# Regrouping the output stage, the edge features and the layer changes of a graph transformer layer

## The chip, the core and the metric

The program runs on one NeuronCore of one Trainium2 chip. The metric is the device time of one execution in microseconds, and a time stands for the median of several executions. All arithmetic is in float32.

## What is computed

One layer of a graph network over N = 3125 nodes with D = 256 features and 100,000 edges, cut here to what matters:

```python
xn = layernorm(x)
# graph part: one message for each edge, summed at its destination
m   = relu(concat(xn[src], edge_attr) @ W1.T + b1)      # edge_attr has 3 columns
hN  = segment_sum(m, dst, N)
gnn = l2norm(relu(concat(xn, hN) @ W2.T))
# mixer: four layers of linear attention and a feed-forward block
for l in range(4):
    h = layernorm(y) * g1 + b1
    q = softmax(h @ Wq, axis=features);  k = softmax(h @ Wk, axis=nodes)
    y = y + (q @ (k.T @ (h @ Wv))) @ Wo + bo
    y = y + gelu(layernorm(y) * g2 @ W1 + b1) @ W2 + b2
x = x + gnn + mix
# expert part: 16 experts, the best 2 for each node
z = layernorm(x)
moe = sum over the 2 best experts e of  gate_e * (relu(z @ w1_e + b1_e) @ w2_e + b2_e)
out = x + layernorm(z + moe) * gamma + beta
```

## The kernel before

Nodes are held as 25 tiles of 125 rows (`xm`, 125 partitions x 25 x 256). Most work runs over seven blocks of tiles, `BLOCKS`: five of 4 tiles, one of 3, one of 2. Block `NB - 1` is the last one.

**Prologue.** For each block the input is normalized (`stage_xn`), a copy in the attention's form is made on ACT (`stage_xh1`), the block is transposed and copied by ACT (`stage_xnT`), and projected by the node part of the edge weights (`stage_proj`), which is stored to `proj` in DRAM. Between these run the first layer's keys and queries.

**Mixer.** The letters of the stages recur in the prediction: `t1` transposes the normalized block, `k` and `q` are the key and query products with their softmax work on DVE and ACT, `ek` and `qT` transpose the exponentials of the keys and the queries, `m` adds the block to the sum `msum` of keys times values. Once all blocks are in `msum`, `context` builds one small matrix `mo` from it, by a chain of four products that depend on each other (mean, its transpose, `ctx`, `mo`). Then `y` adds `qT @ mo` to the nodes, `ln2` and `t2` normalize and transpose, `f1` and `f2` are the feed-forward products, and the next layer's attention stages of the blocks before are woven in. A *change of layer* below is the stretch from the last block's `f2` through `context` to the first `f1` of the next layer. There are four: change 0 (into layer 0, after the prologue), 1, 2 and 3 (into the last layer).

**Edges.** Edges are cut into 784 chunks of 128, and 98 groups of 8 chunks. For a group, GpSimd issues 8 indirect DMAs that gather rows of `proj` (`load_chunk`), SP loads the edge features `ea` in 4 small transfers; `message_step` multiplies the features by a 4-row weight `w1w` on four row strips of the array (8 products, each of 4 rows with 256 columns) and adds the result to the gathered rows (DVE), then Relu (ACT); `sum_step` sums the messages into windows of 32 destinations by a one-hot product and adds the windows of two groups ago to `hNT`. These three kinds of step (0, 1 and 2) stand in a list `due`, with a due place in groups. The list is worked off between the mixer's stages of the first three layers: each stage calls `worked(columns)`, which moves `place` on by `columns * (NG + 1 + LEAD) / total` and runs what has become due. Before a gather, `worked` may issue a one-element copy (`tick`) on GpSimd that waits for the stage's output. Calls of `worked(12 * D)` at a change of layer move `place` without any product of the mixer's own.

PE, ACT and POOL run in the order in which the program is written in the mixer (`manual_schedule`); DVE and SP are ordered by the scheduler.

**Last layer and routing.** The graph part's update (`stage_g`, weights `w2x` and `w2n`) and the gates are woven in. The `slots` tables are written by indirect DMAs.

**Experts.** 37 tiles, 16 of 128 slots and 21 of 256, each with its own expert's weights from SP; each result is scattered by GpSimd to `outs` in DRAM.

**Output.** `outs` is read back in seven parts (four tiles each, then one), the first choice by SP and the second by ACT, each part in two transfers (`by_parts`, 112 and 13 partitions). Identity products on PE sum the two, DVE takes the statistics, and the reciprocal root is worked out in 11 small DVE instructions (`finish_stats`). ACT normalizes, DVE multiplies by gamma, GpSimd adds `xm`, and SP stores. The order on each engine is the scheduler's.

## Time and profile before

| what | value |
|---|---|
| median of 3 runs | 1988.45 us (1987.17 to 1989.06) |
| profiled execution | 1994.73 us, its span 1993.0 us |
| mean granted clock of TensorE | 0.953 |
| PE busy | 1807.7 us, 91% of the span |
| DVE busy | 1165.1 us, 58% |
| POOL busy | 1126.5 us, 57% |
| ACT busy | 743.6 us, 37% |

The span is the time from the first to the last instruction of the profiled execution. Busy is the time in which an engine had an instruction under way; times in which POOL starts a transfer but shows nothing are not in it. The granted clock is TensorE's, as a share of full speed. By stages: the prologue ends at about 130 us, the four changes of layer lie at about 130 to 190, 530 to 650, 950 to 1020 and 1360 to 1420 us, the edges are worked off between 134 and 1363 us, the experts run from about 1690 to 1920 us, and the output stage from 1928 us to the end.

### The profile page before, as it was taken

The numbers are of one execution on the slowest core, as the hardware profiler recorded it, in microseconds if no ns is written. First come the engines' busy times: TensorE is split into PE (matmuls) and PEld (weight loads), VectorE is DVE, ScalarE is ACT, GpSimd is POOL, SyncE is SP. The second block draws the span as 40 slices with busy tenths as digits, with TensorE's granted clock in tenths as the row PEclk, the third lists the DMA queues.
The fourth block names the chain that finished last, engine by engine and source line by source line (L and its number), as shares of the span: only waits on it lengthen the run. The fifth ranks groups of instructions, "written<-read, shape, count | busy, mean of one in ns | idle before, by whom it ended". The sixth has DMA issues, their size and how long they took to land. (4 is left out here: it accounts for less than half of the span.)

```text
span 1993.0 us, 30766 instructions
## 1 busy us (share of the span) xinstructions
PE 1807.7 (91%) x9749; PEld 1269.3 (64%) x9749; DVE 1165.1 (58%) x3761; ACT 743.6 (37%) x1343; POOL 1126.5 (57%) x1429
## 2 busy tenths in 40 slices
PE   6988999999888999999889999998999994999963
PEld 4764656666655666667546666666777783888841
DVE  7654566666664666766656666765646653333326
ACT  3543444344533444544333444443222231222202
POOL 1026777677667777777677777771114435545512
PEclk9998999999988999999889999999999996999987
DMA  6123333233433233334423233333211113777744
GB/s 188 66 77 92 89 85 88 79 88 93 129 98 91 84 93 91 89 84 127 118 81 89 85 90 87 89 89 100 67 29 29 28 19 116 241 259 260 273 130 120
DMA packets 83294, 210.74 MB, mean 106 GB/s; under 512 B 26523, under 2 KB 42306, under 8 KB 78389
## 3 DMA queue, kind: packets, MB, share of 16 engines
q0 software_dynamic: 44800, 118.16, 20.6%
q1 hardware_dynamic: 37246, 87.31, 13.9%
q10 hardware_dynamic: 1078, 3.20, 0.6%
q8 instruction: 84, 1.38, 0.3%
q14 instruction: 86, 0.70, 0.1%
HBM read 187.34 MB, written 21.19 MB: 105 GB/s over the span
## 5 line engine op out<-in xcount | busy, mean ns | idle before, releaser
L255 POOL DMA_INDIRECT gat<-proj,src_i x784 | 761.9, 972 | 212.4 <-issue 163.4
L581 PE MATMUL f_ps<-h2T,ww 128*128 128x500 f32 (+2 forms) x896 | 360.6, 551 | 6.4 <-ACT h2T L339 5.8
L299 ACT ACTIVATE gat<-gat 128x512 f32<-128x512 f32 x392 | 237.6, 630 | 341.0 <-DVE gat L298 315.4
L591 PE MATMUL f_ps<-ww,gT 128*125 128x256 f32 x1600 | 362.3, 382 | 0.0
L298 DVE TENSOR_TENSOR gat<-gat,pw 128x512 f32<-128x512 f32 x392 | 245.5, 680 | 162.1 <-PE pw L294 138.3
L591 PEld LDWEIGHTS f_ps<-ww,gT 128*125 128x125 f32 x1600 | 295.1, 188 | 58.4 <-issue 10.5
L581 PEld LDWEIGHTS f_ps<-h2T,ww 128*128 128x128 f32 x896 | 167.0, 192 | 168.5 <-issue 122.8
L583 ACT ACTIVATE gT<-f_ps,ffb 128x500 f32<-128x500 f32 (+2 forms) x224 | 135.6, 631 | 136.4 <-PE f_ps L581 135.8
L279 PE MATMUL pq<-gat,hot 128*32 128x256 f32 x1568 | 137.6, 405 | 22.4 <-ACT gat L299 22.3
L273 DVE TENSOR_TENSOR hNT<-hNT,win_ps 128x64 f32 x392 | 84.7, 216 | 74.4 <-PE win_ps L270 64.4
L925 POOL DMA_INDIRECT slots<-rec,at x50 | 59.5, 1189 | 110.0 <-DVE rs_u L113 63.7
L596 DVE TENSOR_TENSOR xm<-xm,f_ps 125x512 f32<-125x512 f32 (+1 forms) x52 | 34.7, 667 | 138.7 <-PE f_ps L591 136.4
L1120 PE MATMUL e_ps<-ew,hs 128*128 128x256 f32 x464 | 112.8, 381 | 2.2 <-DVE o L1124 2.2
L294 PE MATMUL pw<-w1w,ea 4*128 4x256 f32 x1568 | 114.6, 403 | 0.0
L1127 POOL DMA_INDIRECT outs<-o,ids x58 | 57.4, 989 | 100.6 <-DVE o L1125 97.5
L458 PE MATMUL q_ps<-wwq,hT 128*125 128x256 f32 x400 | 99.8, 402 | 4.6 <-DVE gat L298 3.6
L563 POOL TENSOR_TENSOR xm<-xm,b 125x1024 f32<-125x1024 f32 (+2 forms) x28 | 59.9, 2140 | 77.6 <-DVE xh L122 58.5
L547 PE MATMUL y_ps<-mo,qT 128*125 128x256 f32 x400 | 98.0, 397 | 4.9 <-DVE mo L538 4.9
L294 PEld LDWEIGHTS pw<-w1w,ea 4*128 4x128 f32 x1568 | 72.5, 185 | 45.0 <-issue 34.5
L495 PE MATMUL m_ps<-xh,ek 125*128 125x257 f32 x400 | 97.9, 398 | 1.8 <-ACT ek L481 1.8
L279 PEld LDWEIGHTS pq<-gat,hot 128*32 128x32 f32 x1568 | 49.6, 112 | 77.9 <-ACT gat L299 45.3
L1120 PEld LDWEIGHTS e_ps<-ew,hs 128*128 128x128 f32 x464 | 85.2, 190 | 20.4 <-issue 4.5
(222 smaller groups left out, 2652.8 us busy)
## 6 DMA issues: line engine op xcount, KB each, us to landing
ew<-ffn_w SPq DMA_DIRECT2D x37, 1154.0 KB
gat<-proj,src_i POOLq DMA_INDIRECT x784
ww<-mix_W SPq DMA_DIRECT2D x8, 1024.0 KB
ea<-eaT SPq DMA_DIRECT2D x392, 4.0 KB
ogs<-outs SPq DMA_DIRECT2D x6, 448.0 KB
ogs<-outs ACTq DMA_DIRECT2D x6, 448.0 KB
out<-ogs SPq DMA_DIRECT2D x6, 448.0 KB
xnT_d<-stage SPq DMA_DIRECT2D x5, 500.0 KB
```

What stands on the lines that cost most here:

```text
L255: nc.gpsimd.indirect_dma_start(out=gats[-1][:, (j // SC) % 2, j % SC, :], out_offset=None, in_=proj, in_offset=bass.IndirectOffsetOnAxis(a ...
L279: nc.tensor.matmul(pq[s * W:(s + 1) * W, :], hot[:, s * SC + i, :], gats[s // 2][:, s % 2, i, :], start=(i == 0), stop=(i == SC - 1))
L294: nc.tensor.matmul(pws[s][:, i, :], ea[s * W:s * W + 4, i * P:(i + 1) * P], w1w[s * W:s * W + 4, :], start=True, stop=True)
L298: nc.vector.tensor_add(msg, msg, pws[s])
L299: nc.scalar.activation(msg, msg, AF.Relu)
L458: nc.tensor.matmul(ps[:, i, :], hT[:, c, cols(o + i)], wt["Wq"][:, c, :], start=(c == 0), stop=(c == KC - 1))
L495: nc.tensor.matmul(ps, st["ek", b][:, i, c * P:(c + 1) * P], xh1s[b % 2][:, i, :], start=(i == 0), stop=(i == n - 1))
L547: nc.tensor.matmul(ps[:, i, :], qT[:, c, cols(t0 + i)], mo[:, c, :], start=(c == 0), stop=(c == KC - 1))
L581: nc.tensor.matmul(ps, wt["W1"][:, c, f * P:(f + 1) * P], st["h2T", b][:, c, :m], start=(c == 0), stop=(c == KC - 1))
L583: nc.scalar.activation(gT[:, f, :m], ps, AF.Gelu, bias=ffb[:, l, f:f + 1])
L591: nc.tensor.matmul(ps[:, i, :], st["gT", b][:, f, cols(o + i)], wt["W2"][:, f, :], start=(f == 0), stop=(f == NF - 1))
L1120: nc.tensor.matmul(ps[:, j, :], x["hs"][:, f, j * P:(j + 1) * P], x["w2"][:, f, :], start=(f == 0), stop=(f == NEF - 1))
```

## The change

It has four parts.

1. Output stage: all loads are issued by SP, in eight parts of 1, 2, 4, 4, 4, 4, 4 and 2 tiles; the root is one ACT instruction, with a reciprocal on DVE; the addition of `xm` goes from GpSimd to DVE; stores are issued by GpSimd; the order on PE, ACT and DVE is the written one, in which a part's multiply, add and store come after the next part's statistics.
2. A group's edge features come as one transfer of 128 x 128, laid out by the host. The two chunks of a strip share one product of 8 rows with 512 columns, whose weight is block-diagonal, so 4 products for a group in place of 8.
3. Order at changes of layer: the last block's `q` moves into `context` of the next layer, its `qT` behind `y` of block 1, and `qT` of the block before it behind `k` of the last. `place` stands still (`held`) from the last block's `f2` to the next layer's first `y`; in that stretch `fill(kind)` runs the next edge step of one kind at four places (from change 1 on), and `total` leaves these columns and the `worked(12 * D)` calls out. In the prologue `stage_xnT` comes ahead of `stage_xh1`.
4. The last expert's half tile is put behind its full tiles, and `w2n` gets a buffer of its own.

```diff
-                ea = edge.tile([P, SC * P], F32, name="ea")
-                for s in range(S):
-                    e0 = (g * S + s) * SC * P
-                    nc.sync.dma_start(ea[s * W:s * W + 4, :], a["eaT"][:, e0:e0 + SC * P])
+                ea = edge.tile([P, P], F32, name="ea")
+                nc.sync.dma_start(ea, a["ea_g"][g])
...
-            for i in range(SC):
-                for s in range(S):
-                    nc.tensor.matmul(pws[s][:, i, :], ea[s * W:s * W + 4, i * P:(i + 1) * P],
-                                     w1w[s * W:s * W + 4, :], start=True, stop=True)
+            for s in range(S):
+                nc.tensor.matmul(pws[s], ea[s * W:s * W + SC * 4, :], w1w[s * W:s * W + SC * 4, :],
+                                 start=True, stop=True)
...
-        total = (DEPTH - 1) * (attention + forward + 60 * D)
+        at_end = sum(len(r) * (2 * KC * TP + KC * D + 2 * KC * P + KC * (D + 1)) for r in BLOCKS[-2:])
+        total = (DEPTH - 1) * (attention + forward) - (DEPTH - 1) * (at_end + BT * KC * D)
+        held = False
...
-            if not spread:
+            if not spread or held:
...
+        def fill(kind):
+            while due and due[-1][1] in (0, kind):
+                _, k, step, i = due.pop()
+                step(i)
+                if k == kind:
+                    return
...
-        def context(l):
+        def context(l, between):
...
+            between[0]()
             ps = mm_tile("meanT_ps").rearrange("p (h m) -> p h m", h=KC)
...
+            between[1]()
             ps = mm_tile("ctx_ps")[:, :D].rearrange("p (c m) -> p c m", c=KC)
...
+            between[2]()
             ps = mm_tile("mo_ps").rearrange("p (c d) -> p c d", c=KC)
...
+            between[3]()
...
             stage_xn(0)
+            stage_xnT(0)
             stage_xh1(0)
-            stage_xnT(0)
...
+            stage_m(0, NB - 1)
             for l in range(last):
                 start_layer(l)
-                context(l)
+                more = (lambda kind: None) if l == 0 else fill
+                context(l, [lambda: stage_q(l, NB - 1), lambda: more(1), lambda: None, lambda: more(2)])
                 load(l + 1, "Wk", "Wq", "Wv")
                 stage_y(l, 0)
+                held = False
                 stage_ln2(0)
                 stage_y(l, 1)
-                worked(12 * D)
+                stage_qT(l, NB - 1)
                 stage_t2(l, 0)
-                worked(12 * D)
...
+                    if b == NB - 1:
+                        stage_ln1(b)
+                        held = True
+                        fill(2)
...
                 stage_ek(l + 1, NB - 2)
-                stage_qT(l + 1, NB - 2)
                 stage_t1(l + 1, NB - 1)
                 stage_m(l + 1, NB - 2)
                 stage_k(l + 1, NB - 1)
-                stage_q(l + 1, NB - 1)
+                stage_qT(l + 1, NB - 2)
                 stage_ek(l + 1, NB - 1)
-                if l + 1 < last:
-                    stage_qT(l + 1, NB - 1)
-                    stage_m(l + 1, NB - 1)
+                fill(1)
+                stage_m(l + 1, NB - 1)
...
-        w2n = wts.tile([P, KC, D], F32, tag="wq", name="w2n")
+        w2n = gates.tile([P, KC, D], F32, name="w2n")
...
-            order += [(i, False)] + [(j, True) for j in range(i * NFS // E, (i + 1) * NFS // E)]
+            full = [(j, True) for j in range(i * NFS // E, (i + 1) * NFS // E)]
+            order += [(i, False)] + full if i < E - 1 else full + [(i, False)]
...
+        def scales(r):
+            tt = slice(r[0], r[-1] + 1)
+            nc.scalar.activation(rs_v[:, tt], mv[:, tt, 1], AF.Sqrt, bias=eps[:, 0:1])
+            return tt
+
+        def normalized(r, tt):
+            nr = tmp.tile([TP, 4], F32, name="nr")
+            nc.vector.reciprocal(rstd[:, tt], rs_v[:, tt])
+            nc.vector.scalar_tensor_tensor(nr[:, :len(r)], mv[:, tt, 0], -1.0, rstd[:, tt], op0=ALU.mult,
                                            op1=ALU.mult)
             for i, t in enumerate(r):
-                nc.scalar.activation(ogs[:, 0, t, :], pss[i], AF.Identity, scale=rstd[:, t:t + 1],
+                nc.scalar.activation(ogs[:, 0, t, :], pss[t], AF.Identity, scale=rstd[:, t:t + 1],
                                      bias=nr[:, i:i + 1])
+
+        def stored(r, tt):
             ys = ogs[:, 0, tt, :]
-            nc.vector.tensor_mul(ys, ys, gamma[:TP, None, :].to_broadcast([TP, n, D]))
-            nc.gpsimd.tensor_add(ys, ys, xm[:, tt, :])
-            by_parts(nc.sync, ov[:, tt, :], ys)
+            nc.vector.tensor_mul(ys, ys, gamma[:TP, None, :].to_broadcast([TP, len(r), D]))
+            nc.vector.tensor_add(ys, ys, xm[:, tt, :])
+            by_parts(nc.gpsimd, ov[:, tt, :], ys)
+
+        with tc.manual_schedule(engines={mybir.EngineType.PE, mybir.EngineType.Activation, mybir.EngineType.DVE}):
+            last = None
+            for r in parts:
+                sums(r)
+                tt = scales(r)
+                if last:
+                    stored(*last)
+                normalized(r, tt)
+                last = r, tt
+            stored(*last)
```

## The prediction

> **What bounds the kernel now.** I read the page's busy times first, then busy time by stretches (columns: stretch, its length, busy time and instructions of PE, PEld, DVE, ACT, POOL, granted clock, DMA share, GB/s), then PE's waits in one change of layer, then the timeline of that change and of the output.

> ```profile
> PE 1807.7 (91%) x9749; PEld 1269.3 (64%) x9749; DVE 1165.1 (58%) x3761; ACT 743.6 (37%) x1343; POOL 1126.5 (57%) x1429
> ...
> 130.00:190.00 60.00, 45.80 (x232) 27.76 (x230) 30.60 (x90) 18.91 (x33) 39.40 (x50) 0.83 0.34 99
> 190.00:530.00 340.00, 329.45 (x1974) 220.15 (x1974) 211.44 (x634) 150.39 (x264) 249.28 (x348) 0.98 0.32 91
> 530.00:650.00 120.00, 98.94 (x566) 61.35 (x559) 71.44 (x222) 44.01 (x79) 80.76 (x107) 0.89 0.35 101
> 950.00:1020.00 70.00, 54.53 (x299) 33.18 (x298) 45.54 (x139) 25.23 (x48) 45.57 (x58) 0.83 0.33 94
> 1360.00:1420.00 60.00, 49.78 (x236) 41.28 (x235) 37.30 (x128) 16.05 (x30) 7.81 (x12) 0.94 0.28 85
> 1920.00:1993.00 73.00, 24.11 (x52) 10.36 (x52) 36.83 (x148) 11.80 (x25) 15.00 (x8) 0.70 0.50 134
> ```

> PE bounds the mixer: between changes of layer it is 97% busy at clock 0.98. At the four changes it idles and its clock falls. The idle is 14.2 + 21.1 + 15.5 + 10.2 = 61 us; busy time at a lower clock, summed over stretches of 10 us, adds 7.7 + 11.1 + 8.9 + 2.3 = 30. So the changes lose 91 us, and the last 73 us of the span hold only 24 us of PE work.

> ```profile
> PE qT_ps L144 <- DVE qs L469: 9.0, 2, 4.9
> PE f_ps L581 <- ACT h2T L339: 4.6, 1, 4.6
> PE pq L279 <- ACT gat L299: 4.0, 4, 2.0
> PE y_ps L547 <- DVE mo L538: 2.1, 1, 2.1
> PE h2T_ps L144 <- DVE xh L122: 1.4, 1, 1.4
> ...
> 574.43 6.64 PE L547 MATMUL y_ps<-mo,qT 128*125 128x256 f32 x16 [2.09 <-DVE mo L538]
> 582.22 3.72 PE L547 MATMUL y_ps<-mo,qT 128*125 128x256 f32 x16
> ```

> These are PE's waits in change 1 (total, times, longest). The largest is the last two `qT` waiting for the softmax of `q` on DVE. The same 16 products took 6.64 us after the stalls and 3.72 us warm.

> ```profile
> 1928.27 24.46 ACTq L74 DMA_DIRECT2D ogs<-outs  x14
> 1938.34 0.76 DVE L90 BATCH_NORM_STATS2 bnst<-sum_ps 125x6 f32<-125x256 f32 x2 [19.32 <-PE sum_ps L1195]
> 1952.92 5.58 ACT L1204 ACTIVATE ogs<-sum_ps,nr,rstd 125x256 f32<-125x256 f32 x12 [42.33 <-DMA ogs<-outs]
> 1956.70 2.98 DVE L1207 TENSOR_TENSOR ogs<-ogs,gamma 125x1024 f32<-125x1024 f32 x1
> 1971.08 1.22 DVE L1207 TENSOR_TENSOR ogs<-ogs,gamma 125x1024 f32<-125x1024 f32 x1
> 1983.71 1.34 SPq L74 DMA_DIRECT2D out<-ogs  x2
> ...
> L255 POOL DMA_INDIRECT gat<-proj,src_i x784 | 761.9, 972 | 212.4 <-issue 163.4
> L294 PE MATMUL pw<-w1w,ea 4*128 4x256 f32 x1568 | 114.6, 403 | 0.0
> ```

> In the output, ACT issues loads until 1952.7 and can't normalize before; DVE then carries the rest, its multiply slowed from 1.22 to about 3 us where GpSimd adds. POOL's gathers (0.97 each, about 0.30 between two) are near a second bound.

> **The change, part by part** (against the profiled 1994.7 us; signs are of time).

> *Prologue, -4.* With `xnT` first, ACT copies the transposes before the four `xh1` copies of a block (0.43 each, 1.7 together). L399 shows about 6 us of PE waiting for that copy; I take 4. `t1` needs `xh1`, but `proj` (16 x 0.2325 = 3.7 us) covers it.

> *Changes of layer, -45.* I count the waits that the new order leaves. Both `qT` waits go: behind `t1`, `m` and `k` (about 5.3 us of PE) the DVE chain of about 5 us is done, and the last `qT` comes 15 us later. What is late next: `ek` waits for `k`'s maximum and exponential, about 2.3 us less `qT`'s 1.0; after `m`, the mean's chain is about 2.2 us against `q`'s 1.9; then the affine of the mean is queued on ACT behind `q`'s exponential, which needs two DVE steps of 0.69, so `ctx` waits about 2.5; `ctxT` 0.75; `t2` about 1 for `ln2`; the first `f1` about 1.5, as the edge work that covered it is gone. With 1 to 2 more at `ln1` that is 9.5 us in changes 1 and 2, 8 in change 0 (14.2 before, part of it waiting for the first gathers), and 5 in change 3, where `stage_g` fills the chain. Clock losses of 3, 3, 3 and 1 remain by the same proportion. Change 0: 21.9 - 11 = 11; changes 1 and 2: 56.6 - 25, of which I leave 4.6 for the `f1` wait behind Relus, a mixer stall that is not touched: 27; change 3: 12.5 - 6 = 6.5. Sum 44.5.

> [...] The trace granted 0.83 in 600 to 610 us, after waits of 0.3 and 2.0 us. [...] I take the row.

> *Edge work packed closer, +8.* `worked` moves 100.25 groups over 579,330 columns now and over 496,536 afterwards. A layer's own products, from spacings in the trace (0.2325 us for 256 columns, 0.44 for 500, 0.14 for a transpose), are 305.6 us for 177,750 columns, 1.72 per thousand. A group takes 2.39 us of PE (1.08 + 1.0 + 0.31). So PE's pace goes from 1.72 x 5.78 + 2.39 = 12.3 to 10.9 us for a group. POOL needs 761.9 (gathers) + 78.6 (ticks) + 44.9 (additions) + 163 (between issues) = 1048 us, 10.7 for a group. It was 87% taken and will be 98% in the free stretches, and while `place` stands still it idles some 25 us a change. The last gather of a group is due 0.75 group, 8 us, ahead of its message, so a lag of 5 to 6 us hides. Stalls such as Relus ahead of an affine (PE lost about 20 us between changes) grow with density, by a fifth: 4, and as much for late gathers. Bounds 0 and 40.

> *Products of edge features, -7.* 16 instructions (two passes each) take 1.15 us for a group, 67 ns apart, on four row strips at once. In the new form 8 instructions stream 512 columns; a 512-column pass is spaced 0.43 us in `sum_ps`, against 2 x 0.2325. A strip then streams 2 x 0.43 instead of 4 x 0.2325: 0.07 less, times 98. If issue were the limit, half of 1.08 would go (-53); if strips overlapped worse, +20. I take the streaming row, the nearest. DVE and ACT work stays.

> *Feature transfers, 0.* SP issues 98 transfers in place of 392 of 0.295 us. Each carries 64 KB, not 16: 4.7 MB more, at a DMA share of 0.33. Gathers and weights share those engines; the features come over a group early (11 us), which hides it.

> *Rest, 0.* `Wq`'s next load waits for the deferred `q`, with `Wv` and later `ea` queued behind it on SP; `q` of the next layer is 60 us away. `w2n` waits for the edge buffers, free about 25 us before its use. The half tile last saves a scatter in the drain but adds its own transposes: 0, bounds -2 and +1.

> *Output, -12.* SP issues 32 loads at about 0.4 us, 13 us beside a transfer of 24.6 us (6.4 MB at 260 GB/s). The first part is 256 KB, not 1 MB: DVE starts at about 1933, not 1938.3. The root's table load (1.28 us, as before Gelu) and first chain cost 2. DVE then has 25 x (0.42 + 0.17) statistics, multiply and add of 7.9 us each, and 2.9 for reciprocals and `nr`: 33.5, more than the loads, so DVE is the bound; with the last normalize (1.5) it ends at about 1970, where it ended at 1980.6. The last addition on POOL (0.7, behind one of 2.3) goes, and two store issues on POOL come (no such row; nearest is the gather, 1.25 each, against SP's 1.34 for both): the last issue ends near 1973, not 1985. That is 12. [...] I keep -12, bounds -4 and -18.

> Sum: -4 - 45 + 8 - 7 - 12 = -60, so 1935 for such a profiled execution. That execution stands 6.3 us above the median; from the median, 1988.4 - 60 = 1928.

> **Rivals.** *Half* (0.2): the closer edges keep POOL late, PE waits for Relus of late gathers, the clock falls again. For: POOL at 98%. Against: waits for gathers were 45 us on DVE and ACT together in all, mostly at changes. It costs half of the change gain (22) and 12 more of density: 1962.

> *POOL becomes the bound* (0.09), the slower side. In the free stretches PE would need 98 x 10.9 = 1068 us. POOL fits only while a gather costs at most about 1.27 us, issue to issue. At 1.45 us (ticks or DVE sharing delay each by 0.2), POOL needs 1048 + 784 x 0.2 = 1205, 137 more than PE's time: 1928 + 137 - the 16 gathers a change done by `fill` (40) = 2025. It turns slower than before above about 1.40, where the 60 us of gain, 40 and the slack of 20 are spent. Against: gathers are 0.97 + 0.30 now at any DVE load.

> *More* (0.1): issue bounds the feature products and most waits vanish; then POOL's time sets the end, near 1890.

> *Nothing* (0.02): the stalls move one for one.

> **Numbers.** The likeliest case (0.59) gives 1928, its own range 1905 to 1952. The range 1893 to 1972 holds nearly all of it, most of *half* and some of *more*. Within 0.2% (4 us) is about what a measurement of this kernel can tell from no change. Faster 0.89, same 0.02, slower 0.09.

> **What would show it.** Right: no `qT` wait for `qs`; four changes with about 30 us of idle; POOL nearly gapless between them; pw near 1.08 us a group; ACT normalizing by 1936; no multiply of 3 us; last store issued some 12 us earlier after the last scatter. Wrong: gathers more than 1.3 us apart, `pq` waiting for Relus throughout, or stores on POOL over 3 us each.

## The result and the profile after

The changed kernel takes 1954.4 us (median of 4 runs, 1949.1 to 1959.8), the kernel before 1987.8 (1986.8 to 1989.1): a ratio of 0.983, 95% interval 0.980 to 0.986. That is 33.5 us less, where I had forecast 60 less (1928); the range of 1893 to 1972 holds it. The profiled execution took 1957.5 us, with a span of 1955.8, so its span is 37.2 us under that of before.

First the busy times and the stretches of the kernel after, cut at its own changes of layer and closer than those of before (236 us in all, there 310; columns as before: stretch, length, busy time of PE, PEld, DVE, ACT, POOL, granted clock, DMA share, GB/s).

```profile
PE 1808.7 (92%) x8965; PEld 1225.8 (63%) x8965; DVE 1162.5 (59%) x3696; ACT 748.9 (38%) x1352; POOL 1116.4 (57%) x1413
...
126.00:170.00 44.00, 34.75 (x132) 24.10 (x131) 19.71 (x69) 10.19 (x19) 10.12 (x14) 0.84 0.19 56
170.00:530.00 360.00, 351.22 (x1902) 217.75 (x1901) 232.61 (x688) 169.03 (x295) 292.93 (x400) 1.00 0.38 109
530.00:592.00 62.00, 51.55 (x204) 31.58 (x203) 35.91 (x111) 18.82 (x35) 17.68 (x21) 0.83 0.18 53
592.00:934.00 342.00, 337.24 (x1840) 211.04 (x1839) 227.59 (x661) 159.07 (x282) 277.88 (x382) 1.00 0.37 105
934.00:990.00 56.00, 45.61 (x186) 30.85 (x188) 37.72 (x122) 18.12 (x33) 15.48 (x17) 0.79 0.24 73
990.00:1326.00 336.00, 329.61 (x1778) 201.99 (x1774) 217.66 (x647) 157.80 (x277) 267.53 (x360) 0.99 0.35 101
1326.00:1400.00 74.00, 63.16 (x299) 50.81 (x292) 43.82 (x156) 18.60 (x36) 7.58 (x12) 0.95 0.30 92
1895.00:1956.00 61.00, 24.99 (x52) 9.81 (x52) 30.97 (x83) 14.54 (x33) 9.54 (x17) 0.77 0.57 163
```

PE does the same 1808 us of busy time with fewer instructions. Between the changes it is 98% busy at clock 0.99 to 1.00, with the edge work packed closer. At the four changes it idles 9.3 + 10.5 + 10.4 + 10.8 = 41 us, where it idled 61. Busy time at a lower clock (busy times one minus the clock) is 5.6 + 8.8 + 9.6 + 3.2 = 27 us, where it was 30. So nearly all that was won at the changes is idle, and hardly any clock.

Change 1 in PE's timeline (start, length, engine, line, operation, in brackets the wait ahead of it and who ended it):

```profile
551.49 0.49 PE L537 MATMUL ctx_ps<-meanT,wwv 128*128 128x128 f32 x2 [2.19 <-ACT meanT L348]
...
554.37 2.08 PE L546 MATMUL mo_ps<-wwo,ctxT 128*128 128x256 f32 x4 [0.52 <-DVE ctxT L541]
556.38 2.09 PE L292 MATMUL pw<-w1w,ea 8*128 8x512 f32 x8
558.39 9.10 PE L557 MATMUL y_ps<-mo,qT 128*125 128x256 f32 x32
...
570.65 1.42 PE L144 MATMUL h2T_ps<-ident,xh 125*128 125x125 f32 x8 [2.73 <-DVE xh L122]
...
575.13 9.91 PE L591 MATMUL f_ps<-h2T,ww 128*128 128x500 f32 x18 [0.39 <-DVE h2T L350]
```

Both waits of `qT` for the softmax are gone, as forecast. No wait in this change is over 2.8 us. Yet behind the wait of 2.19 us all products come at half speed: `mo` takes 2.08 us, `pw` 2.09, and the 32 of `y` 9.10. The timelines of other kernels below have 1.13, 1.14 and 7.17 for these. After the wait of 2.73 the first `f1` products are slow again.

The granted clock in stretches cut there shows the same thing directly: 10 us at half speed after a wait of 2.2.

```profile
552.00:556.00 4.00, 3.28 (x10) 2.53 (x10) 1.43 (x4) 0.00 (x0) 0.00 (x0) 0.51 0.20 63
...
560.00:562.00 2.00, 2.00 (x7) 1.52 (x6) 0.96 (x2) 1.63 (x3) 0.00 (x0) 0.50 0.04 7
562.00:566.00 4.00, 4.00 (x19) 3.48 (x18) 3.51 (x12) 0.00 (x0) 0.00 (x0) 0.96 0.00 0
```

The output stage, from its timeline, and two of the page's groups, the gathers and the feature products:

```profile
1904.39 24.09 SPq L74 DMA_DIRECT2D ogs<-outs  x32
...
1938.37 1.23 DVE L1235 TENSOR_TENSOR ogs<-ogs,gamma 125x1024 f32<-125x1024 f32 x1
1939.63 1.22 DVE L1236 TENSOR_TENSOR ogs<-ogs,xm 125x1024 f32<-125x1024 f32 x1
1952.44 0.53 POOL L74 DMA_DIRECT2D out<-ogs  x1 [2.70 <-issue]
```

```profile
L254 POOL DMA_INDIRECT gat<-proj,src_i x784 | 761.4, 971 | 189.1 <-issue 141.1
...
L292 PE MATMUL pw<-w1w,ea 8*128 8x512 f32 x784 | 122.0, 649 | 0.5 <-DVE qs L474 0.4
```

From the first output load to the end of the span it is 51.4 us, where it was 64.8. DVE multiplies and adds in 1.23 and 1.22 us each, and no multiply takes 3 any more. The gathers still take 0.97 us each. The 98 groups of feature products were meant to be cheaper, and their busy time is not lower: 122.0 after 114.6.

The span cut at points that all kernels share (the first `y` of each layer, the first transpose of the experts, the first output load), in us. The kernels other than before and after are those of the experiments:

| | start to y(0) | y(0) to y(1) | y(1) to y(2) | y(2) to y(3) | y(3) to experts | experts to loads | loads to end | span |
|---|---|---|---|---|---|---|---|---|
| before | 153.3 | 421.2 | 416.7 | 414.6 | 283.6 | 239.1 | 64.8 | 1993.0 |
| after | 145.8 | 412.6 | 408.0 | 411.8 | 288.3 | 237.9 | 51.4 | 1955.8 |
| e1 output alone | 154.1 | 420.2 | 412.7 | 414.4 | 283.4 | 237.9 | 50.5 | 1973.4 |
| e2 edges alone | 149.3 | 416.5 | 416.6 | 407.3 | 283.2 | 237.9 | 65.3 | 1976.3 |
| e3 order alone | 143.0 | 413.3 | 411.2 | 415.5 | 288.5 | 237.9 | 63.1 | 1972.4 |
| e4 q put back | 142.6 | 413.0 | 407.4 | 413.6 | 287.5 | 237.7 | 51.3 | 1953.2 |
| e9 after, other chip | 143.4 | 503.6 | 490.9 | 481.3 | 287.1 | 237.8 | 51.0 | 2195.1 |
| e10 waits filled, same chip as e9 | 144.7 | 502.7 | 477.4 | 477.6 | 287.2 | 237.9 | 51.3 | 2178.7 |
| e12 edge steps in the waits, same chip as e9 | 153.4 | 486.3 | 479.6 | 479.3 | 289.3 | 237.4 | 50.2 | 2175.3 |

Each row is one execution: that of e2 lies 5 us under the median of its kernel, that of e12 10 us above. A layer of e1, whose mixer is that of before, differs from before by up to 4 us, so that much in one cell is chance. On the other chip layers vary more, for reasons that are not known.

### The profile page after: what moved, and what is told of

It reads as the page before. It is cut to its first block, busy times and chain, and to the rows that moved or that the text cites. A ratio compares the mean times of both kernels' runs of the same rounds, so it can differ in the third digit from the quotient of the medians.

```text
span 1955.8 us, 28486 instructions
## 1 busy us (share of the span) xinstructions
PE 1808.7 (92%) x8965; PEld 1225.8 (63%) x8965; DVE 1162.5 (59%) x3696; ACT 748.9 (38%) x1352; POOL 1116.4 (57%) x1413
## 3 DMA queue, kind: packets, MB, share of 16 engines
q8 instruction: 77, 1.26, 0.3%
## 5 line engine op out<-in xcount | busy, mean ns | idle before, releaser
L591 PE MATMUL f_ps<-h2T,ww 128*128 128x500 f32 (+2 forms) x896 | 367.4, 559 | 7.1 <-ACT h2T L348 6.2
L297 DVE TENSOR_TENSOR gat<-gat,pw 128x512 f32<-128x512 f32 x392 | 250.8, 677 | 173.1 <-PE pw L292 157.0
L278 PE MATMUL pq<-gat,hot 128*32 128x256 f32 x1568 | 123.7, 388 | 9.0 <-ACT gat L298 8.5
L292 PE MATMUL pw<-w1w,ea 8*128 8x512 f32 x784 | 122.0, 649 | 0.5 <-DVE qs L474 0.4
L441 PE MATMUL k_ps<-hT,wwk 128*128 128x500 f32 (+2 forms) x224 | 92.9, 558 | 5.9 <-DVE hT L350 5.2
L467 PE MATMUL q_ps<-wwq,hT 128*125 128x256 f32 x400 | 93.5, 384 | 4.5 <-DVE gat L297 2.8
L557 PEld LDWEIGHTS y_ps<-mo,qT 128*125 128x125 f32 x400 | 79.3, 203 | 25.1 <-issue 7.2
```

The costliest lines, as they stand in the source:

```text
L278: nc.tensor.matmul(pq[s * W:(s + 1) * W, :], hot[:, s * SC + i, :], gats[s // 2][:, s % 2, i, :], start=(i == 0), stop=(i == SC - 1))
L292: nc.tensor.matmul(pws[s], ea[s * W:s * W + SC * 4, :], w1w[s * W:s * W + SC * 4, :], start=True, stop=True)
L297: nc.vector.tensor_add(msg, msg, pws[s])
L467: nc.tensor.matmul(ps[:, i, :], hT[:, c, cols(o + i)], wt["Wq"][:, c, :], start=(c == 0), stop=(c == KC - 1))
L557: nc.tensor.matmul(ps[:, i, :], qT[:, c, cols(t0 + i)], mo[:, c, :], start=(c == 0), stop=(c == KC - 1))
L591: nc.tensor.matmul(ps, wt["W1"][:, c, f * P:(f + 1) * P], st["h2T", b][:, c, :m], start=(c == 0), stop=(c == KC - 1))
```

## The experiments

Theory: the change does what it says at the waits, but what remains of them (2 to 4 us each) still halves the clock for 7 to 10 us, so the term for the clock was too small. Rivals: one of the other parts (edges, output) fell short; the closer edge work took the gain back; or what was moved into the chain (the deferred softmax) made new waits.

### The three parts alone

```diff
e1: + ogs held from before the experts; all loads on SP, parts of 1, 2, 4, ... tiles
    + root on ACT, both passes on DVE, stores on GpSimd   (mixer as before)
e2: - for i in range(SC): for s in range(S): matmul(pws[s][:, i, :], ea[...4 rows], w1w[...4 rows])
    + for s in range(S): matmul(pws[s], ea[...SC*4 rows], w1w[...SC*4 rows])
    + ea from one transfer of ea_g[g]
e3: + prologue, held, fill, total, moves of q, qT, m, w2n   (edges and output as before)
```

> The kernel before with the output stage of the change alone (all loads issued by SP, stores by GpSimd, root on ACT, both vector passes on DVE). My prediction: 12 us less than before, so about 1976. The trace after shows the stretch from the first output load to the end of the span at 51.4 us, where it was 64.7: by it 13 us less, about 1975. Rival, that part of the gain came from the earlier layout of the experts ahead of it: 8 us or less, 1980 or more.

Measured: 1975.0 us against 1993.1 for before on the same chip, ratio 0.992 (0.990 to 0.994), so 12 to 21 us less, and 18 by the medians. The tail is 14 us shorter in the table, and no other cell differs by more than chance. The forecast of 12 lies at the lower edge; the rival (8 or less) is out, so the stage needs nothing of the other parts for its gain. In its timeline the last store is issued 47.1 us after the first load (1969.94 and 1922.85), as in the kernel after (48.0).

> The kernel before with the edge features in one transfer and eight matmuls of 512 columns in place of sixteen of 256 for a group. My prediction: 7 us less, about 1981. Rival, read from the trace after, where the products of a group take 1.07 us from start to start and not 1.08: no more than 1 to 2 us less, 1986 to 1988, since what bounds these eight is not the columns of a row strip. A third, that the padded transfers or the wider waits cost: above 1990.

Measured: 1983.3, ratio 0.996 (0.994 to 0.997), so 5 to 11 us less. The number that I forecast (7) came out and the reason did not. From the first product of a group to the next instruction on PE it is 1.071 us (median), where it was 1.076: over 98 groups half a microsecond. What differs stands in PE's waits. Those ahead of `pq` for a Relu are 19.6 us in all, where they were 22.3, which is no clear difference, since e1 with the mixer of before has 20.4. Those of `h2T` for DVE's additions (total, times, longest over the whole run), first of before, then of this kernel:

```profile
PE h2T_ps L144 <- DVE gat L298: 7.1, 4, 1.9
```

```profile
PE h2T_ps L144 <- DVE gat L297: 1.9, 6, 0.8
```

These are 5 us smaller, and e1 has 7.1 like before. A reason for it lies in the loops: before, the four `pw` tiles of a group were finished together, as `i` was the outer loop; now the first is finished after a quarter of the products. DVE's first addition follows the first product by 1.16 us (median) instead of 1.43, and the last Relu of the group ends 0.18 us sooner. That such a small shift makes the whole gain is argued, not shown. The profiled execution also had a higher clock (0.956) than the kernel's other runs (0.950 to 0.951), so a part of what its trace saves is chance.

> The kernel before with the new order alone (prologue, the moves of q, qT and m at the changes of layer, held and fill, the pace, w2n in a buffer of its own). My prediction's terms: 4 of the prologue, 45 of the changes, 8 back for edge work packed closer, so 41 less: 1947. Rival, read from the trace after (idle at the changes as forecast, granted clock still lost there): about 20 less, 1968. If the two other parts together explain less than 12, this one would have to give more than 22.

Measured: 1974.8, ratio 0.992 (0.990 to 0.994), so 13 to 21 us less. My 41 is out, and the reading of the trace (20) holds. This is the part that fell short. In the table the start and the first two layers gain 10, 8 and 6 us, the third none, and the stretch from `y(3)` to the experts loses 5. The chain of change 1 has the same waits as in the kernel after, and the same slow products:

```profile
549.40 0.49 PE L538 MATMUL ctx_ps<-meanT,wwv 128*128 128x128 f32 x2 [2.19 <-ACT meanT L349]
...
556.24 9.25 PE L558 MATMUL y_ps<-mo,qT 128*125 128x256 f32 x32
```

The product of the three ratios is 0.980; the whole change gave 0.983 (0.980 to 0.986) on another chip. So the parts add within their intervals, and no large loss comes from their being together. The half tile of the last expert is in none of the three; the stretch of the experts is 237.9 us in all of them and in the kernel after, so it is worth nothing that can be seen.

### The deferred q put back

```diff
                 stage_k(l + 1, NB - 1)
+                stage_q(l + 1, NB - 1)
                 stage_qT(l + 1, NB - 2)
...
-                context(l, [lambda: stage_q(l, NB - 1), ...])
+                context(l, [lambda: None, ...])
```

> The kernel after, with q of the last block put back behind its k (as before), while its qT stays behind the second y. The later q lies beside the mean's chain and hides it; its softmax then stands on DVE ahead of the next ln2. Theory A (the deferred softmax is what makes the waits of 2.2 us for the affine of the mean and of 2.7 to 3.9 us for ln2): these waits fall to about 0.7 and 1.2 us, but PE waits about 2 us for the mean instead; four changes give 5 to 10 us less than after, 1945 to 1949. Theory B (the 1.9 us of q hid the mean and are only paid elsewhere): within 3 us of after, 1951 to 1957, with the wait for the mean as large as those taken away. Slower than 1958 would say that q in the chain was worth more than its softmax cost.

Measured: 1950.7 (1944.0 to 1954.9), ratio 0.978 (0.976 to 0.980), so about 10 us less than the kernel after by the ratio of the two ratios, with an interval of some 7 either way, as the two were run on different chips. Change 1 in PE's timeline:

```profile
550.13 0.72 PE L530 MATMUL meanT_ps<-ident,mean 128*128 128x128 f32 x4 [1.25 <-DVE mean L525]
551.50 1.51 PE L537 MATMUL ctx_ps<-meanT,wwv 128*128 128x128 f32 x8 [0.65 <-ACT meanT L348]
553.54 1.13 PE L546 MATMUL mo_ps<-wwo,ctxT 128*128 128x256 f32 x4 [0.52 <-DVE ctxT L541]
...
555.67 7.17 PE L557 MATMUL y_ps<-mo,qT 128*125 128x256 f32 x32
...
566.29 1.76 PE L144 MATMUL h2T_ps<-ident,xh 125*128 125x125 f32 x8 [3.02 <-DVE xh L122]
```

Half of theory A holds. The wait of `ctx` falls from 2.19 to 0.65, a wait of 1.25 for the mean comes in its place, and here these short waits leave the clock up: `y` takes 7.17 us instead of 9.10. In change 2 the same waits (1.26, 0.65 and 0.52) do not: `y` takes 8.73. The wait for `xh` does not fall (3.02), so the deferred softmax is not its cause: with `q` out of the way, the chain from `y` through the statistics, `ln2` and its four normalizations is that long by itself, and the edge steps that stood in it before (there 1.39 was left) are no longer there. In the last change it is 3.5 us with and without.

### The waits filled with products that nothing uses

```diff
+        def warm(n):
+            for _ in range(n):
+                nc.tensor.matmul(mm_tile("warm")[:, :500], ident, qT[:, 0, :500], start=True, stop=True)
 ...  (ahead of ctx, not in the last change)
+            warm(4)      # e6; e10: warm(2)
 ...  (ahead of the first stage_t2 of each layer)
+                warm(6)      # e6; e10: warm(3)
e7: the same places, each product replaced by three 128x128 transposes
```

These kernels compute the same and do more work. They and the kernel after ran on two other chips, where the kernel before takes 2227 us (e5 to e8) and 2209 us (e9 to e12), so they are compared with the kernel after on the same chip.

> The kernel after itself, beside the three that follow on the same chip. Both theories expect its ratio to the kernel before to be the one measured already, 0.983, give or take 0.003. If it is nearer 0.979, as the product of the three parts run alone (0.992 x 0.996 x 0.992), the parts add and the first comparison was on the high side; if it stays at 0.983, 5 to 8 us of the parts are lost when they are together.

Measured: 2207.9, ratio 0.992 (0.988 to 0.995). On this chip PE loses time in the main stretches of the kernel after (about 485 to 510 us for a layer instead of 412). The kernel before is longer by about as much in all (239 us, the kernel after 254), but no trace of it was kept here. Why what the change saves is less on this chip, and whether the parts add, can't be read from it.

> The kernel after, with matmuls that nothing uses (128x128 by 500 columns, 0.44 us each) laid into the two longest waits of each change of layer: four ahead of ctx (wait of 2.2 us; not in the last change) and six ahead of the first h2T transposes (waits of 2.7 to 3.9 us). They add no work to what is computed. Theory A (these waits, though under 4 us, are what makes the clock fall, and a busy TensorE keeps it up): the clock of the four changes rises from 0.83, 0.83, 0.79 and 0.95 to 0.93 and more, the y and f1 products behind the waits come at their warm pace (0.23 and 0.44 us each); of the 27 us of clock loss 10 to 15 come back: 8 to 15 us under the kernel after. Rival B (the clock falls with the whole thin stretch, whatever stands in these two waits): same clock, 0 to 5 us slower than after.

Measured: 2209.1, ratio 0.992 (0.989 to 0.995), no different from the kernel after. I had mis-sized the filler: a product took 0.88 us, being two passes, so 3.5 and 5.2 us stood in waits of 2.2 and 2.7 to 3.9. The clock did what theory A says: `y` took 7.17 us in the first three changes, where the kernel after had 8.7 to 9.9 on this chip. From the transposes of the mean to the twelfth `f1` pass the three changes took 26.4, 27.9 and 29.6 us against 29.7, 31.2 and 32.6. So each was 3 us shorter, and the total does not show these 10 us: its runs spread over 2199 to 2220. This run settles the clock, and nothing for the time.

> The same as the kernel with matmuls in the waits, but with groups of three 128x128 transposes instead (0.14 us each, so 0.42 for a group): four groups ahead of ctx, six ahead of h2T. Theory A1 (any TensorE instruction keeps the clock): same gain as with matmuls, 8 to 15 us under the kernel after. Theory A2 (transposes do not count, so the wait for ctx, which has transposes of the mean ahead of it, looks longer to the throttle than it is): clock at the changes as in the kernel after (0.79 to 0.84), time within 3 us of it or up to 5 above.

Measured: 2203.6, ratio 0.989 (0.986 to 0.993): 5 us under the kernel after, with an interval that holds zero. The `y` of the first two changes was warm (7.17), that of the third partly cold (8.55), with 0.9 us of wait left after the transposes in the second and third. So the run alone does not settle whether transposes keep the clock; a count over all traces, below, suggests that they do.

> The kernel after itself, as the measure for the three that follow: 0.983 of before, give or take 0.003, as in the first comparison; 0.992 if this chip is again the one where the kernel before takes 2227 us.

Measured: 2198.0, ratio 0.994 (0.992 to 0.996), near the 0.992 of the other slow chip. It serves as the measure for the next three.

> The kernel after with unused matmuls in the two long waits of each change, now sized by the trace: a product of 128x128 by 500 columns took 0.88 us (two passes), so two ahead of ctx (1.76 us in a wait of 2.2) and three ahead of the first h2T (2.6 us in waits of 2.7 to 3.9). Theory A (the clock falls for a wait of 2 us or more, and what is lost is the slow products behind it: mo 2.07 in place of 1.13 us, y 9.3 to 9.9 in place of 7.17, the first 20 passes of f1 10.5 to 10.9 in place of 8.7): 3 us to 6 us less for each change, 10 to 18 us under the kernel after in all. Rival B (what is saved there comes back as waits for gathers or Relus in the main stretch, or the idle was not on the path): 0 to 4 us under it.

Measured: 2180.6, ratio 0.987 (0.984 to 0.990): 17 us under the kernel after on the same chip, in the range that theory A gave (10 to 18), and far from rival B. Change 1 of the kernel after on this chip, and then of this one:

```profile
640.83 0.49 PE L537 MATMUL ctx_ps<-meanT,wwv 128*128 128x128 f32 x2 [2.19 <-ACT meanT L348]
...
647.04 9.89 PE L557 MATMUL y_ps<-mo,qT 128*125 128x256 f32 x32
...
660.09 1.95 PE L144 MATMUL h2T_ps<-ident,xh 125*128 125x125 f32 x8 [2.72 <-DVE xh L122]
662.69 10.51 PE L591 MATMUL f_ps<-h2T,ww 128*128 128x500 f32 x20 [0.65 <-ACT h2T L348]
```

```profile
640.73 1.84 PE L519 MATMUL warm<-qT,ident 128*128 128x500 f32 x4
643.08 0.49 PE L543 MATMUL ctx_ps<-meanT,wwv 128*128 128x128 f32 x2 [0.51 <-ACT meanT L348]
...
646.31 1.14 PE L292 MATMUL pw<-w1w,ea 8*128 8x512 f32 x8
647.38 7.17 PE L563 MATMUL y_ps<-mo,qT 128*125 128x256 f32 x32
...
654.82 2.68 PE L519 MATMUL warm<-qT,ident 128*128 128x500 f32 x6
658.01 1.42 PE L144 MATMUL h2T_ps<-ident,xh 125*128 125x125 f32 x8 [0.51 <-DVE xh L122]
...
662.50 7.81 PE L597 MATMUL f_ps<-h2T,ww 128*128 128x500 f32 x18 [1.31 <-DVE h2T L350]
```

The producers of `meanT` and `xh` are as late as ever; PE only has something to do meanwhile. The granted clock from 645 to 655 us is 0.62 in the first and 1.00 in the second kernel:

```profile
645.00:655.00 10.00, 10.00 (x33) 7.01 (x33) 6.27 (x14) 2.42 (x4) 0.00 (x0) 0.62 0.16 48
```

```profile
645.00:655.00 10.00, 9.75 (x49) 7.67 (x50) 8.31 (x27) 2.42 (x4) 0.00 (x0) 1.00 0.31 75
```

From the transposes of the mean to the twelfth `f1` pass it is 26.1 us in each of the first three changes, where the kernel after has 30.2, 31.2 and 30.8: 14 us in all, beside 17 in the total, while doing 4.5 us more work in each. In the last change the filler changes nothing (34.9 and 34.9). So the clock behind waits of 2 to 4 us costs 4 to 5 us a change, and this is the term that I mis-sized. The table does not split the total in the same way: the stretch from y(1) to y(2) is 13.5 us shorter, that from y(0) to y(1) only 0.9, and the main stretches on this chip vary by several us. That the whole 17 us come from the changes is therefore not shown; the 14 inside the changes are.

> The kernel after with q of the last block back behind its k (which leaves waits of 1.25 us for the mean and 0.65 us for its affine in place of 2.2), and three unused products of 0.88 us ahead of the first h2T alone. Theory A (any wait below about 1.5 us leaves the clock up, so here only the h2T wait has to be filled): 4 to 8 us under the kernel that has q put back alone (0.978 of before), so 0.974 to 0.976, and the best of these. Rival: the clock falls for the sum of short waits, and the result stays at 0.978.

Measured: 2186.1, ratio 0.990 (0.986 to 0.993): 12 us under the kernel after on the same chip by the medians, no more than `q` put back seemed to give alone (about 10). Theory A is wrong in its threshold. In change 1 waits of 1.26, 0.66 and 0.52 us, the same as where the clock had stayed up, cost the clock this time:

```profile
632.68 2.00 PE L541 MATMUL ctx_ps<-meanT,wwv 128*128 128x128 f32 x8 [0.66 <-ACT meanT L348]
...
639.22 9.41 PE L561 MATMUL y_ps<-mo,qT 128*125 128x256 f32 x32
```

So no single wait length decides. In changes 0 and 2 of this very execution nearly the same waits (1.38 or 1.26, then 0.66 and 0.52) leave the clock up, with `y` at 7.17.

The clock record of the traces shows what does decide. In all fourteen the granted clock is either 0.50 or 1.00, and it changes only at points of a grid of 3.413 us, which starts at another time in every execution. What counts is how much PE has done within one such window. In change 1 of e11 the waits fall into one window, in which PE is busy for 1.50 of 3.41 us (the number behind the length of the stretch), and the next window runs at half speed:

```profile
630.14:633.55 3.41, 1.50 (x8) 1.04 (x9) 1.76 (x5) 0.56 (x1) 0.00 (x0) 1.00 0.00 0
633.55:636.96 3.41, 2.89 (x10) 2.01 (x9) 0.42 (x1) 0.00 (x0) 0.00 (x0) 0.50 0.25 77
```

In change 1 of e4 the grid cuts the chain elsewhere, so the same waits are shared by two windows with 2.00 and 2.14 us of work, and the clock stays:

```profile
546.38:549.79 3.41, 2.00 (x8) 1.44 (x8) 2.39 (x8) 0.71 (x2) 0.00 (x0) 1.00 0.00 0
549.79:553.20 3.41, 2.14 (x12) 1.49 (x12) 1.15 (x4) 0.56 (x1) 0.00 (x0) 1.00 0.00 0
553.20:556.62 3.42, 3.08 (x16) 1.85 (x17) 1.83 (x4) 0.14 (x1) 0.00 (x0) 1.00 0.51 124
```

The wait of 2.19 us in the kernel after leaves 1.12 us of work in the window from 548.67 us, and three windows of half speed follow, 10.24 us. With two products in that wait, e10 has 2.91 and 2.66 us of work in the two windows there, and keeps full speed. Over all windows at full speed in the fourteen traces, the next window was at half speed after every one of the 216 in which PE was busy for under 40%, after 194 of 426 between 40 and 70%, and after 70 of 6824 above. The share of busy time is thus not the whole measure: change 2 of e4 lost the clock after 2.16 us. Counting the columns of all recorded matmul passes, each weighted with the share of the 128 array rows that it uses, parts the windows better: half speed followed 318 of 319 windows with under 1200 such columns and 11 of 6841 with over 1800. With the transposes left out of the count, a single limit puts 211 of 7440 windows on the wrong side; with them in it, 73. So transposes seem to count as work here. All of this is read from the traces; no run was made to test it. (The 7440 leave out each trace's first windows.)

### Edge work put back into the waits

```diff
-        def fill(kind):                       # one step of this kind, if it is next
+        def fill(*kinds):                     # one step of these, and place += 0.5
-            place += columns * (NG + 1 + LEAD) / total
+            place += columns * (NG + 1 + LEAD - 7) / total
+    a step while the mean is made, behind mo, and behind the last qT ahead of t2, in all changes
+    q back behind its k; in the last change y of the second block between ln2 and t2
```

> The kernel after, with q of the last block back behind its k, and with edge work that has to be done anyway put into the waits: one step (sums or messages) at each of five places of a change (behind the last f2, ahead of m, while the mean is made, behind mo, ahead of the first h2T), counted in the pace; in the last change y of the second block covers ln2 in place of half a product of the update. Theory (waits of 2 us and more are what costs the clock, and edge steps both cover them and are taken from the main stretch): the waits for xh fall under 1.5 us, clock at the changes 0.9 and more, 8 to 15 us under the kernel with q put back alone (0.978 of before), so 0.971 to 0.974 of before. Rival (the steps' own Relus and copies stand on DVE and ACT ahead of the chain and make it later, as the deferred softmax did): within 4 us of 0.978.

> The kernel with real edge steps in the waits of a change, again, since on the chip of its first run waits of 3 to 8 us, which no other run has, stood between its steps. Theory (a step needs gathers and Relus of its own, so it covers a wait only where these are in time): xh waits near 1 us and y at 7.2 us, 8 us under the kernel after at least; the first f1 waits behind the Relus of the step put ahead of it by 1 us or more. Rival (the Relus stand ahead of the chain on ACT and DVE): within 4 us of after or slower.

Measured: 2191.8 (0.984, 0.981 to 0.987) beside the kernel after at 2207.9, and 2167.1 (0.979, 0.976 to 0.982) beside 2198.0. So it is 16 and 31 us under the kernel after, and the fastest kernel on both chips. It was not run on a chip where the kernel before takes 1988 us, so its time there is open. Its theory holds only in part. In change 1 of e12 `y` is warm (7.17) and the wait for `xh` is 1.02, but in the first and last change the wait for `xh` is 6.0 and 4.9; and in change 1 the affine of the first `h2T` waits on ACT behind the Relus of the step put ahead of it, 8.55 us, where I had said 1 or more. That Relu was late because the last of the step's four additions on DVE had to wait for its gather to land:

```profile
658.35 0.69 DVE L297 TENSOR_TENSOR gat<-gat,pw 128x512 f32<-128x512 f32 x1 [2.35 <-DMA gat<-proj,src_i]
659.07 0.63 ACT L298 ACTIVATE gat<-gat 128x512 f32<-128x512 f32 x1 [4.98 <-DVE gat L297]
...
660.65 3.44 PE L592 MATMUL f_ps<-h2T,ww 128*128 128x500 f32 x4 [8.55 <-ACT h2T L349]
```

So a step covers a wait only where its gathers are in time, as the theory had it, and the changes themselves are longer than in the kernel after. The gain is in what the layers no longer hold: in the table the first two layers take 17 and 11 us less than in e9, and the start 10 more. How much of it is the thinner main stretch and how much the `q` put back, these runs do not tell.

## Why the prediction was right, and where it was wrong

It was right in sign and within its range, at a little over half of the size. The largest term was off by half, and that the total still came so near is in part luck: a cost of 8 us that I had set against it did not come. Point by point, against the profiled execution:

- **Changes of layer, forecast -45.** This is the step that failed. The new order did what I worked out for the idle, roughly: 9.3, 10.5, 10.4 and 10.8 us against the forecast of 8, 9.5, 9.5 and 5. The failing term is "Clock losses of 3, 3, 3 and 1 remain by the same proportion": they are 5.6, 8.8, 9.6 and 3.2. So 68 us are lost at the changes, not 42, and the part gave 91 - 68 = 23. The clock is not lost in proportion to idle time: at the changes of the traces before and after, a window of 3.41 us with too little work in it was followed by one to three windows at half speed (3.41 to 10.24 us). Waits of 4.9 and 4.1 us for the softmax went from change 1, waits of 2.2 and 2.7 came, and each still left such a window. The filled waits of e10 show by experiment that the waits are the cause. About 10 us (with an interval of 7 either way) come back when `q` stays where it was (e4), so deferring it was a part of the loss.
- **The idle terms themselves.** `ctx` at 2.5 us was 2.2. The wait for `ln2`, put at "about 1", was 2.7 to 3.9: I let `qT` and `y` of the second block cover it and did not count that the edge work which `worked(12 * D)` used to place there had covered it. (In before 1.39 us were left.) The last change, put at 5 with `stage_g` as its cover, was 10.8, of which 2.3 is a wait for a Relu ahead of the chain and 3.5 the wait for `xh`.
- **The row that was taken.** The row of the trace before (clock 0.83 in 600 to 610 us, after waits of 0.3 and 2.0 us) says that short waits cost clock. It was right, and should have been taken further: with it this part was -45, by the profile after -23. In the fourteen traces the clock changes on a grid of 3.413 us that starts at another time in each, and a window of it need not be idle to cost clock: the one from 548.67 us of the trace after holds 1.12 us of work, and 216 of 216 windows with PE busy for under 40% were followed by one at half speed. So the work in each window was the thing to count, not the length of a wait.
- **Prologue, -4.** PE's wait for the copy of `proj` fell from 6.9 to 3.7 us, but the wait for DVE's half of the first `hT`, in front of the second half of `k`, grew from 2.5 to 5.2. The first `proj` starts 1.7 us earlier, the second block 1.0 later (32.80 after 31.77), and the last `proj` is 0.8 ahead (125.8 after 126.6). So the term was worth about 1; the other 6.7 us to `y(0)` are change 0.
- **Edge work packed closer, +8.** On the chips of the first comparison no cost appears: 98.1% busy (1018 of 1038 us) at clock 0.99 to 1.00 in the free stretches, and 0.97 us for a gather. PE's waits for Relus ahead of `pq` fell from 22 to 9 us. On the two other chips the kernel that thins this stretch again is the fastest; since it changes other things too, that does not show a cost there, but the zero is shown for the first chips alone.
- **Feature products, -7.** The total came out (5 to 11 less in e2), by another way than a shorter stream: the products take the same 1.07 us. That is luck.
- **Output, -12.** Measured -13 in the whole and -14 in e1, in the stage's own stretch. DVE is the bound, as worked out: from 1916.6 to 1942.2 us it is busy for 23.5 of 25.6 us. The stores on GpSimd took 1.04 to 1.17 us for two, where I had taken 1.25 for each from the gathers. They are issued about 0.5 us after DVE's additions (one ends at 1926.30, the store starts at 1926.84). Only one pair runs beside a multiply, and that for 0.17 us (1946.29 to 1947.33, the multiply from 1947.16), so what a multiply does to a store is not shown.
- **From y(3) to the experts, not in my sum:** +5, in e3 too. `qT` of the last block (0.6) now stands behind `y(3)`, and PE waits 3.5 us for `xh` with a slow `y` after it. How it splits was not tested.

Put together: 60 less 22 of the changes, 3 of the prologue and 6 of the products, plus 8 that the edges did not cost and 1 of the output is 38, beside 37 measured between the two spans. That these meet proves little: the products are put at 1 there and what e2 gained in waits is counted with the edges, and the three parts alone gave 18, 10 and 18 us by their medians on another chip, 46 where the whole gave 33.5. Of the rivals *half* came nearest in time (1962), by the clock that it named but not by its cause: PE did not wait for late gathers. *POOL becomes the bound* did not come. Its limit of 1.27 us for a gather was set too high besides: by the prediction's own terms it is (1068 - 79 - 45) / 784 = 1.20, and the gathers took 0.97 and 0.18 between two.

## What to carry to other kernels

When a chain of small steps interrupts a dense TensorE stretch, count its waits and what each costs in clock behind it, not only their sum. Here waits of 4.9 us gave way to waits of 2.2 and 2.7, and the clock loss hardly changed (30 and 27 us); filling those waits brought back 4 to 5 us a change. What to look at is the work in each window of 3.41 us: in these traces under 40% busy cost the clock every time (216 of 216), over 70% hardly ever (70 of 6824). Filler has to fit: twice the size won nothing in time. Before work is moved out of such a chain, ask which wait it was covering; the edge steps between `y` and the first `h2T` had been hiding most of `ln2`. And where a part of the gain comes out right, look whether it came by the path that was worked out: the feature products did not get faster, their consumers only started sooner.

## What the runs showed of the hardware

```profile
ACT osb L281 <- remote: 117.2, 15, 13.6
```

- **A plain store issued by GpSimd** took about 0.53 us in the trace after (1.04 to 1.17 for two), less than the 0.97 of its gathers.
